# A 3x3 convolution with residual: combined images pair columns instead of rows

## The chip, the cores and the metric

The kernel runs on one core of a Trainium2 chip. The metric is the device time of one launch in microseconds (us); lower is better. TensorE (PE) does the matmuls, with its weight loads shown as PEld; VectorE is DVE, ScalarE is ACT, GpSimd is POOL, and SP issues most of the DMAs.

## What is computed

There are 160 images of 128 channels and 32 x 32 pixels. Each is normalised in groups of four channels, convolved with a 3x3 kernel of 128 x 128 channels, and added to itself. There are five sets of weights; 32 images use each. The weights are first quantised in two steps.

```python
s1 = (beta - alpha) / 3.0
v1 = s1 * floor(U / s1)
s2 = s1 / 5.0
v2 = s2 * floor((U - v1) / s2)
w = (v1 + v2).reshape(OUT_CH * N, IN_CH, 3, 3)
xb = x.reshape(B // N, N * C, H, W)
act = conv_general_dilated(xb, w, strides (1, 1), padding 1, groups N)
...
m = mean(g, axis=(2, 3, 4)); s = var(g, axis=(2, 3, 4))   # 32 groups
gn = (g - m) / sqrt(s + 1e-5)
...
x = x + conv(gn(x), U)
```

## The kernel before

The weights are whole numbers in fp16; an image is split into a high and a low fp16 part, and both are multiplied. Channels lie on the 128 partitions. An image's output fills two PSUM banks of 512 fp32 each (`eo`), the upper and the lower 16 rows.

The convolution saves products along the rows. For a pair of neighbouring output rows three vertical taps (g0, g1, g2) need four products instead of six: two "main" ones on differences of rows two apart (with g0 and with -g2), and two "sums", of g0+g1+g2 with the sum of a row pair and of g0-g1+g2 with its difference. Each product is made once for each of the three columns of taps, with the image shifted by one column, so two of three matmuls work on rows of 31. The sums of image i+1 go to the banks `m1a` or `m1b` and `m2`, ahead of image i's main part. `leave` copies `m2` to SBUF on ACT, `pairs` writes m1+m2 and m1-m2 into the rows of a new `eo` on DVE, and the main products are then accumulated on top. Taps are stored doubled, so `eo` holds twice the result, and `residual` halves it.

There are two kinds of image from the seventh on. In a **plain** image the high part is convolved directly (`taps`, L660: 9 taps x 2 halves = 18 matmuls); only the low part takes the short way (L699: 12 main products of 8 rows each, 6 sums). In a **combined** image differences and sums are made from the raw fp32 image into `v` of 2048 elements (`outer_rows` on POOL for the two edge rows, `combine` on DVE for the rest), scaled and split afterwards into `vh` (ACT, L607) and `vl` (DVE, L613); both parts take the short way: 24 main products and 12 sums, 36 matmuls, as many as the 18 + 12 + 6 of a plain image. There are 82 combined images and 75 plain ones of this kind; the first three use taps alone. Up to image 126 the two kinds alternate.

The order on every engine is written out by hand in `run`: an iteration i holds the sums of i+1 and the main part of i on PE, the low part of i+2, the normalisation of i+3 and the edge rows of i+4, then `pairs` of i+1 and `combine` of i+4 on DVE. Statistics of later images run on ACT (L194, L201), with short chains on POOL (L220 to L245). `residual` on ACT (L788) evacuates `eo` into `sum`, and POOL issues a DMA that adds `sum` to the image in SBUF (L807); 23 images take one DVE instruction instead (L799). Weights of the next set are quantised on DVE a step at a time; a finished column of taps is turned on PE (`turn_column`), copied by ACT (`keep_taps`, `keep_halves`) and combined by POOL (`keep_sums`). The products' matmul is a single line:

```python
self.nc.tensor.matmul(
    target[:, :, c0:c1],
    self.wts[n, col][:, kind, :],
    source[:, :, c0 + dw : c1 + dw],
```

Of the kernel before, what the change touches and what calls it, by code (L numbers as in the profile page):

```python
# [33 lines left out]
class Steps:  # L34
# [61 lines left out]
    def nearest(self, pool, v, parts, name, dt, by_scalar=False):  # L96

        tag = "ns" if by_scalar else "nn"
        n = pool.tile(list(v.shape), dt, tag=tag, name=f"{tag}_{name}")
        engine = self.nc.scalar.mul if by_scalar else self.nc.vector.tensor_scalar_mul  # L100
        engine(n, v, parts[0])
        return n
# [208 lines left out]
class Main:  # L311
# [35 lines left out]
    G, SUM, DIFF, MINUS_G2 = slice(0, 3), 3, 4, 5  # L347

    def __init__(self, tc, ctx, keep, x, u, out):
# [41 lines left out]
        self.wts = {}  # L391
# [91 lines left out]
    def keep_taps(self, n, col):  # L483

        P = self.P
        wt = self.wpool.tile([P, 6, P], MM, tag=f"wt{col}", name=f"wt{n}_{col}")
        self.nc.scalar.mul(wt[:, self.G, :], self.pt, 2.0 / LIFT)  # L487
        self.wts[n, col] = wt

    def keep_halves(self, n, col):  # L490
        half = self.qpool.tile([self.P, ROW, self.P], MM, tag="half", name=f"half{n}_{col}")
        self.nc.scalar.mul(half, self.pt, 1.0 / LIFT)
        return half

    def keep_sums(self, n, col, half):

        nc, P, wt = self.nc, self.P, self.wts[n, col]
        outer = self.qpool.tile([P, P], MM, tag="outer", name=f"outer{n}_{col}")
        nc.gpsimd.tensor_tensor(outer, half[:, 0, :], half[:, 2, :], ALU.add)
        nc.gpsimd.tensor_tensor(wt[:, self.SUM, :], outer, half[:, 1, :], ALU.add)  # L500
        nc.gpsimd.tensor_tensor(wt[:, self.DIFF, :], outer, half[:, 1, :], ALU.subtract)
        nc.gpsimd.tensor_scalar_mul(wt[:, self.MINUS_G2, :], wt[:, 2, :], -1.0)

    def keep_column(self, n, col):
        self.keep_taps(n, col)
        self.keep_sums(n, col, self.keep_halves(n, col))
# [71 lines left out]
    def outer_rows(self, i):  # L578

        nc, P, H, W = self.nc, self.P, self.H, self.W  # L580
        st, j = self.column_of(i)
        v = self.v[i] = self.wide.tile([P, 2048], F32, tag="v", name=f"v{i}")
        x = self.image(i)
        minus, last = st.ngm[:, j], (H - 1) * W
        nc.gpsimd.tensor_scalar(v[:, :W], x[:, W : 2 * W], minus, -1.0, ALU.add, ALU.mult)  # L585
        nc.gpsimd.tensor_scalar(
            v[:, last : H * W], x[:, last - W : last], minus, 1.0, ALU.add, ALU.mult
        )

    def combine(self, i):  # L590


        nc, H, W = self.nc, self.H, self.W
        st, j = self.column_of(i)
        v, x, last = self.v[i], self.image(i), (H - 1) * W
        nc.vector.tensor_sub(v[:, W:last], x[:, : last - W], x[:, 2 * W :])  # L596
        pairs = x.rearrange("p (i a w) -> p a i w", a=2, w=W)
        s, t = (v[:, k : k + 512].rearrange("p (i w) -> p i w", w=W) for k in (1024, 1536))
        nc.vector.scalar_tensor_tensor(
            s, pairs[:, 0], st.twice[:, j], pairs[:, 1], ALU.add, ALU.add  # L600
        )
        nc.vector.tensor_sub(t, pairs[:, 1], pairs[:, 0])  # L602
# [24 lines left out]
    def combinations(self, i):  # L627


        nc, P, H, W = self.nc, self.P, self.H, self.W  # L630
        lo = self.los[i % len(self.los)]
        rows = self.v[i] = self.rows.tile([P, 2048], MM, tag="rows", name=f"rows{i}")
        d, st = self.halves(rows)
        yield nc.vector.tensor_sub(d, lo[:, 0:H, :], lo[:, 2 : H + 2, :])
        pairs = lo[:, 1 : H + 1, :].rearrange("p (i a) w -> p a i w", a=2)
        yield nc.vector.tensor_add(st[:, 0], pairs[:, 0], pairs[:, 1])
        yield nc.vector.tensor_sub(st[:, 1], pairs[:, 1], pairs[:, 0])

    def halves(self, v):

        return (
            v[:, :1024].rearrange("p (h w) -> p h w", w=self.W),
            v[:, 1024:].rearrange("p (a i w) -> p a i w", a=2, w=self.W),
        )

    def taps(self, i, part, col, target, last, halves=(0, 1)):
# [7 lines left out]
        for k in (1, 0, 2):  # L654
            for h in halves:

                h0 = h * (H // 2)
                r0, r1 = max(h0, 1 - k), min(h0 + H // 2, H + 1 - k)
                s0 = r0 + k - 1 + top
                nc.tensor.matmul(  # L660
                    self.bank(target, h)[:, r0 - h0 : r1 - h0, c0:c1],
                    self.wts[n, col][:, k, :],
                    tile[:, s0 : s0 + r1 - r0, c0 + dw : c1 + dw],
                    start=(i < self.FIRST and col == self.COLS[0] and k == 1 and top == 0),
                    stop=(last and k == 2),
                    skip_group_check=True,
                )
# [17 lines left out]
    def direct_hi(self, i, col):  # L685
# [3 lines left out]
        self.taps(i, (self.hi[i], 0), col, self.eo[i], False)  # L689

    def direct_lo(self, i, col):
        lo = self.los[i % len(self.los)]
        self.taps(i, (lo, 1), col, self.eo[i], col == self.COLS[-1])

    def product(self, target, i, kind, source, col, start, stop):
        n, _ = self.place(i)
        dw = col - 1
        c0, c1 = max(0, -dw), self.W - max(0, dw)
        self.nc.tensor.matmul(  # L699
            target[:, :, c0:c1],  # L700
            self.wts[n, col][:, kind, :],
            source[:, :, c0 + dw : c1 + dw],
            start=start,
            stop=stop,
            skip_group_check=True,
        )
# [4 lines left out]
    def both(self, i):  # L711

        return [self.halves(v) for v in ([self.hi[i]] if self.combined(i) else []) + [self.v[i]]]

    def sums_of_pairs(self, i):

        both = self.both(i)
        for a, kind in ((1, self.DIFF), (0, self.SUM)):
            for col in self.COLS:
                for j, (_, st) in enumerate(both):  # L720
                    self.product(
                        self.m2_ps if a else self.m1(i), i, kind, st[:, a], col,
                        col == self.COLS[0] and j == 0,
                        col == self.COLS[-1] and j == len(both) - 1,
                    )

    def conv(self, i, on_the_way):
# [4 lines left out]

        for halves in ((0,), (1,)) if i == self.imgs - 1 else ((0, 1),):
            for col in self.COLS:
                if col == self.COLS[2] and i == self.FIRST:
                    self.sums_of_pairs(i + 1)
                if col != self.COLS[0] and halves[-1] == 1:
                    on_the_way(col)
                self.rest_of_column(i, col, halves)
        del self.v[i]  # L740

    def rest_of_column(self, i, col, halves):
        eo, both = self.eo[i], self.both(i)
        if not self.combined(i):
            self.taps(i, (self.hi[i], 0), col, eo, False, halves)
        for a, kind in enumerate((0, self.MINUS_G2)):
            for j, (d, _) in enumerate(both):
                for h in halves:
                    rows = slice(h * 16 + a, h * 16 + 16, 2)
                    to = eo[:, h].rearrange("p (i a) w -> p a i w", a=2)[:, a]  # L750
                    self.product(
                        to, i, kind, d[:, rows, :], col, False,
                        col == self.COLS[-1] and a == 1 and j == len(both) - 1,
                    )

    def leave(self, i):

        m2 = self.evac.tile([self.P, self.H // 2, self.W], F32, tag="m2", name=f"m2_{i}")
        self.nc.scalar.copy(m2, self.m2_ps)  # L759
        self.m2[i] = m2  # L760

    def pairs(self, i, between=lambda: None):
# [5 lines left out]
        rows = eo.rearrange("p h (i a) w -> p (h i) a w", a=2)  # L768
        nc.vector.tensor_add(rows[:, :, 0], m1, m2)  # L769
        between()  # L770
        nc.vector.tensor_sub(rows[:, :, 1], m1, m2)  # L771
# [8 lines left out]
    def residual(self, i):  # L780
# [5 lines left out]
        if not self.by_hand(i):  # L786
            self.sum[i] = self.sums.tile([self.P, 1024], F32, tag="sum", name=f"sum{i}")
            nc.scalar.mul(self.sum[i], eo.rearrange("p h r w -> p (h r w)"), 0.5)  # L788
            return
        xj = self.image(i)  # L790
        if i == self.imgs - 1 or eo is self.pair:
            parts = [
                (slice(h * 512, h * 512 + 512), self.bank(eo, h).rearrange("p r w -> p (r w)"))
                for h in range(2)
            ]
        else:
            parts = [(slice(0, 1024), eo.rearrange("p h r w -> p (h r w)"))]
        for h, part in parts:
            nc.vector.scalar_tensor_tensor(  # L799
                xj[:, h], part, 0.5, xj[:, h], ALU.mult, ALU.add  # L800
            )
            if i >= self.imgs - LAST:
                nc.sync.dma_start(self.ov[n, :, b, h], xj[:, h])
# [12 lines left out]
    def run(self):  # L816
# [120 lines left out]
        half = self.keep_halves(0, self.COLS[2])  # L937
        self.stats[2].deviations()
        self.keep_sums(0, self.COLS[2], half)
# [5 lines left out]
        for i in range(self.imgs):  # L945
# [58 lines left out]
            else:  # L1004
# [14 lines left out]
                if self.combined(i + 4):  # L1019
                    self.outer_rows(i + 4)  # L1020
# [98 lines left out]
```

## Time and profile before

| | |
|---|---|
| Time, median of 3 runs | 989.86 us (989.83 to 991.1) |
| Span of the profiled execution | 988.9 us (its own time isn't listed apart from the three above) |
| PE busy | 955.3 us, 97%, 5938 matmuls |
| PEld busy | 577.8 us, 58% |
| DVE busy | 933.8 us, 94%, 1259 instructions |
| ACT busy | 891.7 us, 90%, 1219 instructions |
| POOL busy | 414.9 us, 42%, 569 instructions |
| Mean DMA rate | 249 GB/s |
| Mean granted TensorE clock | 0.998 |

The busy shares are of the span. A busy PE is not PE at its peak: matmuls are pipelined, and their ends are modelled, so a matmul's price is read from the distance between starts or from the chain of waits, not from its duration. Groups of instructions are named by line, engine, output and inputs; idle time stands behind the bar, with what ended it.

### The profile page before, as it was taken

Reading aid. Unit: us, or ns where it says so; the run is one execution under the profiler, and the core shown is the slowest. Engines: PE = TensorE matmul, PEld = TensorE weight load, DVE = VectorE, ACT = ScalarE, POOL = GpSimd, SP = SyncE. Lnnn points to the kernel's source line nnn. Section 1 sums busy time; section 2 is a strip of 40 time slices with the busy share of each in tenths; the row PEclk is TensorE's granted clock in tenths of the full one; section 3 lists DMA queues with packets and bytes.
Section 4 is the critical chain, followed back from the end, with each engine's and each line's share of the span. In section 5 each row is a group of like instructions: output and inputs, shape, how many; then the busy total and the mean of one; then the engine's idle time right before and its main releaser. Section 6 shows DMA issues by size and latency. Waiting matters only on the chain.

```text
span 988.9 us, 16124 instructions
## 1 busy us (share of the span) xinstructions
PE 955.3 (97%) x5938; PEld 577.8 (58%) x5938; DVE 933.8 (94%) x1259; ACT 891.7 (90%) x1219; POOL 414.9 (42%) x569
## 2 busy tenths in 40 slices
PE   2899999999999999999999999999999999999997
PEld 1445656566656566666666666666665556666664
DVE  7999999999999999999999999999999999989995
ACT  5779999899999999999999999999999999998651
POOL 4435564634416273514343736415343544332410
PEclk9999999999999999999999999999999999999999
DMA  9538999999997989998998898998999899987764
GB/s 360 209 104 235 238 251 280 252 267 266 268 302 183 296 215 297 267 288 243 271 239 267 224 274 232 315 271 246 233 280 301 212 293 224 298 231 207 184 177 153
DMA packets 65129, 246.05 MB, mean 249 GB/s; under 512 B 5008, under 2 KB 5008, under 8 KB 65040
## 3 DMA queue, kind: packets, MB, share of 16 engines
q1 hardware_dynamic: 45312, 173.09, 50.3%
q0 software_dynamic: 19728, 71.84, 37.7%
q8 instruction: 48, 0.79, 0.3%
q14 instruction: 41, 0.34, 0.1%
HBM read 89.19 MB, written 83.89 MB: 175 GB/s over the span
## 4 chain that ended last, share of the span: by engine, by line
PE 66%; ACT 12%; DVE 10%; issue 5%; POOL 3%; DMA 3%; SPq 0%; DVEq 0%; ACTq 0%; POOLq 0%
PE eo L699 22%; PE eo L660 21%; PE m L699 11%; PE m1b L699 7%; PE m1a L699 4%; ACT junk L201 3%; ACT vh L607 3%; ACT sum L788 2%; ACT z L538 1%; DVE v L596 1%; DMA xt<-sum 1%; ACT m L759 1%; DVE vl L613 1%; DVE eo L769 1%; POOL v L585 1%
## 5 line engine op out<-in xcount | busy, mean ns | idle before, releaser
L699 PEld LDWEIGHTS <-wt 128*128 128x128 f16 x4302 | 420.4, 98 | 236.5 <-issue 4.1
L660 PE MATMUL eo<-hi,wt 128*128 128x496 f16 (+3 forms) x1386 | 331.0, 375 | 1.6 <-ACT wt L487 0.9
L807 POOL DMA_DIRECT2D xt<-sum x137 | 122.8, 906 | 441.1 <-ACT sum L788 426.9
L660 PEld LDWEIGHTS <-wt 128*128 128x128 f16 x1458 | 142.5, 99 | 138.4 <-DVE eo L771 2.3
L613 DVE SCALAR_TENSOR_TENSOR vl<-v,rstd,vh 128x2048 f16<-128x2048 f32 x82 | 192.9, 2352 | 1.9 <-ACT vh L607 1.9
L699 PE MATMUL eo<-vh,wt 128*128 128x248 f16 (+1 forms) x984 | 188.5, 273 | 0.0
L699 PE MATMUL eo<-vl,wt 128*128 128x248 f16 (+1 forms) x984 | 188.5, 273 | 0.0
L194 ACT ACTIVATE junk<-xt 128x1024 f16<-128x1024 f32 x152 | 160.6, 1057 | 18.0 <-DMA xt<-in_x_dram 14.2
L201 ACT ACTIVATE junk<-xt,mv 128x1024 f16<-128x1024 f32 x152 | 173.8, 1143 | 0.1
L607 ACT ACTIVATE vh<-v,rstd 128x2048 f16<-128x2048 f32 x82 | 164.8, 2009 | 4.7 <-DVE v L602 2.4
L788 ACT ACTIVATE sum<-eo 128x1024 f32<-128x1024 f32 x137 | 138.2, 1008 | 14.0 <-PE eo L699 14.0
L699 PE MATMUL eo<-rows,wt 128*128 128x256 f16 (+1 forms) x900 | 135.3, 273 | 0.0
L759 ACT COPY m<-m 128x512 f32<-128x512 f32 x157 | 90.7, 578 | 19.2 <-PE m L699 19.1
L538 ACT ACTIVATE z<-xt,shift,rstd 128x1024 f32<-128x1024 f32 x75 | 93.6, 1248 | 3.5 <-POOL shift L243 3.4
L620 DVE TENSOR_TENSOR lo<-z,hi 128x1024 f16<-128x1024 f32 x78 | 95.6, 1225 | 0.0
L699 PE MATMUL m<-vl,wt 128*128 128x496 f16 (+1 forms) x246 | 93.4, 380 | 1.1 <-DVE vl L613 1.1
L699 PE MATMUL m<-vh,wt 128*128 128x496 f16 (+1 forms) x246 | 93.4, 380 | 1.0 <-ACT m L759 1.0
L596 DVE TENSOR_TENSOR v<-xt 128x960 f32<-128x960 f32 x82 | 94.3, 1150 | 0.0
L585 POOL TENSOR_SCALAR v<-xt,ngm 128x32 f32<-128x32 f32 x82 | 90.7, 1106 | 0.1
L553 ACT CAST hi<-z 128x1024 f16<-128x1024 f32 x78 | 81.6, 1046 | 2.3
L699 PE MATMUL m1b<-vh,wt 128*128 128x496 f16 (+1 forms) x213 | 80.9, 380 | 0.0
L699 PE MATMUL m1b<-vl,wt 128*128 128x496 f16 (+1 forms) x213 | 80.9, 380 | 0.0
(129 smaller groups left out, 1210.0 us busy)
## 6 DMA issues: line engine op xcount, KB each, us to landing
xt<-in_x_dram SPq DMA_DIRECT2D x78, 1024.0 KB, 9.5
out_dram<-xt SPq DMA_DIRECT2D x78, 1024.0 KB, 5.9
xt<-sum POOLq DMA_DIRECT2D x137, 512.0 KB, 6.5
u<-in_L_conv_U_dram SPq DMA_DIRECT2D x4, 576.0 KB, 9.6
xt<-in_x_dram SPq DMA_DIRECT2D x4, 512.0 KB, 9.6
range<-in_L_conv_U_dram SPq DMA_DIRECT2D x3, 576.0 KB, 7.8
out_dram<-xt SPq DMA_DIRECT2D x3, 512.0 KB, 2.8
u<-in_L_conv_U_dram SPq DMA_DIRECT2D x2, 288.0 KB, 2.9
```

Of the source, the lines that this page charges most:

```text
L194: self.nc.scalar.activation(junk, image, ACTF.Copy, scale=-1.0 / image.shape[1], accum_out=self.mv[:, j, 0:1],)
L201: self.nc.scalar.activation(junk, image, ACTF.Square, bias=self.mv[:, j, 0:1], accum_out=self.mv[:, j, 1:2],)
L538: nc.scalar.activation(z, self.image(i), ACTF.Identity, bias=st.shift[:, j : j + 1], scale=st.rstd[:, j : j + 1],)
L585: nc.gpsimd.tensor_scalar(v[:, :W], x[:, W : 2 * W], minus, -1.0, ALU.add, ALU.mult)
L596: nc.vector.tensor_sub(v[:, W:last], x[:, : last - W], x[:, 2 * W :])
L607: self.nc.scalar.mul(vh, self.v[i], st.rstd[:, j])
L613: self.nc.vector.scalar_tensor_tensor(vl, self.v[i], st.rstd[:, j], self.hi[i], ALU.mult, ALU.subtract)
L660: nc.tensor.matmul(self.bank(target, h)[:, r0 - h0 : r1 - h0, c0:c1], self.wts[n, col][:, k, :], tile[:, s0 : s0 + r1 - r0, c0 + dw : c1 + ...
L699: self.nc.tensor.matmul(target[:, :, c0:c1], self.wts[n, col][:, kind, :], source[:, :, c0 + dw : c1 + dw], start=start, stop=stop, skip_g ...
L759: self.nc.scalar.copy(m2, self.m2_ps)
L788: nc.scalar.mul(self.sum[i], eo.rearrange("p h r w -> p (h r w)"), 0.5)
L807: self.nc.gpsimd.dma_start(self.image(i), self.sum.pop(i), accum_op=ALU.add)
```

## The change

Combined images now pair neighbouring columns, with the three rows of taps as the shifts. `v` is stored so that a quarter (even outputs, odd outputs, sums, differences) holds 32 rows of 16 column pairs; a shift by one row is then a shift by 16 elements, and a shifted product is one contiguous run of 496. The weights of sums and differences across columns are a new tile, `across`, made once for each set when its last column is kept. Plain images keep pairing rows, but the two banks of `eo` now hold even and odd output rows (for combined images: columns) instead of halves, so that a main product fills a whole bank. The sign of the odd differences moves from the weights into the differences. The taps are stored plain, not doubled; the factor of a half goes into `leave` and `pairs`. `residual` puts even and odd outputs back in their places as it evacuates. The last image's products are ordered by bank, and it is stored after both banks.

```diff
     def keep_taps(self, n, col):
-        wt = self.wpool.tile([P, 6, P], MM, ...)
-        self.nc.scalar.mul(wt[:, self.G, :], self.pt, 2.0 / LIFT)
+        wt = self.wpool.tile([P, 5, P], MM, ...)
+        self.nc.scalar.mul(wt[:, self.G, :], self.pt, 1.0 / LIFT)
...
-    def keep_halves(self, n, col):
-        half = self.qpool.tile([self.P, ROW, self.P], MM, ...)
-        self.nc.scalar.mul(half, self.pt, 1.0 / LIFT)
-        return half
...
-        nc.gpsimd.tensor_tensor(outer, half[:, 0, :], half[:, 2, :], ALU.add)
-        nc.gpsimd.tensor_tensor(wt[:, self.SUM, :], outer, half[:, 1, :], ALU.add)
-        nc.gpsimd.tensor_tensor(wt[:, self.DIFF, :], outer, half[:, 1, :], ALU.subtract)
-        nc.gpsimd.tensor_scalar_mul(wt[:, self.MINUS_G2, :], wt[:, 2, :], -1.0)
+    def both_sums(self, total, diff, g0, g1, g2):
+        pool = self.nc.gpsimd
+        pool.tensor_tensor(total, g0, g2, ALU.add)
+        pool.tensor_tensor(diff, total, g1, ALU.subtract)
+        pool.tensor_tensor(total, total, g1, ALU.add)
+    def keep_sums(self, n, col):
+        wt = self.wts[n, col]
+        self.both_sums(wt[:, self.SUM], wt[:, self.DIFF], *(wt[:, k] for k in range(ROW)))
+        if col == self.COLS[-1]:
+            across = self.wpool.tile([self.P, 2, ROW, self.P], MM, ...)
+            self.across[n] = across
+            self.both_sums(
+                across[:, 0], across[:, 1], *(self.wts[n, c][:, self.G] for c in range(ROW))
+            )
...
-        nc.gpsimd.tensor_scalar(v[:, :W], x[:, W : 2 * W], minus, -1.0, ALU.add, ALU.mult)
-        nc.gpsimd.tensor_scalar(
-            v[:, last : H * W], x[:, last - W : last], minus, 1.0, ALU.add, ALU.mult
-        )
+        self.nc.gpsimd.tensor_scalar(
+            self.view(v, 0, (512 + W // 2 - 1, 2), (W // 2, H)),
+            self.view(self.image(i), 1, (W - 3, 2), (W, H)),
+            st.ngm[:, j], -1.0, ALU.add, ALU.mult,
+        )
...
-        nc.vector.tensor_sub(v[:, W:last], x[:, : last - W], x[:, 2 * W :])
-        nc.vector.scalar_tensor_tensor(
-            s, pairs[:, 0], st.twice[:, j], pairs[:, 1], ALU.add, ALU.add
-        )
-        nc.vector.tensor_sub(t, pairs[:, 1], pairs[:, 0])
+        nc.vector.tensor_tensor(
+            self.view(v, 1, (511, 2), (half, H), (1, half - 1)),
+            self.view(x, 1, (1, 2), (W, H), (2, half - 1)),
+            self.view(x, 3, (-3, 2), (W, H), (2, half - 1)),
+            ALU.subtract,
+        )
+        even, odd = (x[:, a::2] for a in range(2))
+        nc.vector.scalar_tensor_tensor(
+            v[:, 1024:1536], even, st.twice[:, j], odd, ALU.add, ALU.add
+        )
+        nc.vector.tensor_sub(v[:, 1536:], odd, even)
...
     def product(self, target, i, quarter, step, kind, start=False):
+        for j, source in enumerate(self.both(i)):
+            source = source[:, quarter * 512 : quarter * 512 + 512]
+            if self.combined(i):
+                weights = self.across[n][:, kind - self.SUM, step] if kind >= self.SUM else (
+                    self.wts[n, kind][:, step]
+                )
+                out, half = target.rearrange("p i w -> p (i w)"), W // 2
+                first, end = max(0, -shift) * half, 512 - max(0, shift) * half
+                out, moving = out[:, first:end], source[:, first + shift * half : end + shift * half]
...
+    def main(self, i, a, between=lambda: None):
+        to = self.bank(self.eo[i], a)
+        for step in self.KS:
+            if step == self.KS[1] and a == 1 or step == self.KS[2] and a == 0:
+                between()
+            if not self.combined(i):
+                self.taps(i, (self.hi[i], 0), step, self.eo[i], (a,))
+            self.product(to, i, a, step, 2 * a)
...
-        self.nc.scalar.copy(m2, self.m2_ps)
+        self.nc.scalar.mul(m2, self.m2_ps, 0.5)
...
-        nc.vector.tensor_add(rows[:, :, 0], m1, m2)
+        nc.vector.scalar_tensor_tensor(eo[:, 0], m1, 0.5, m2, ALU.mult, ALU.add)
         between()
-        nc.vector.tensor_sub(rows[:, :, 1], m1, m2)
+        nc.vector.scalar_tensor_tensor(eo[:, 1], m1, 0.5, m2, ALU.mult, ALU.subtract)
...
+    def as_banks(self, i, image):
+        if self.combined(i):
+            return image.rearrange("p (q a) -> p a q", a=2)
+        return image.rearrange("p (i a w) -> p a i w", a=2, w=self.W)
...
-            nc.scalar.mul(self.sum[i], eo.rearrange("p h r w -> p (h r w)"), 0.5)
+            nc.scalar.copy(self.as_banks(i, self.sum[i]), self.flat(i, eo))
...
+            for a, quarters in ((0, (slice(0, 512),)), (1, (slice(0, 256), slice(256, 512)))):
+                for h, q in enumerate(quarters):
+                    nc.vector.tensor_add(image[:, a, q], banks[:, a, q], image[:, a, q])
+                    if a == 1:
+                        half = slice(h * 512, h * 512 + 512)
+                        nc.sync.dma_start(self.ov[n, :, b, half], xj[:, half])
```

Three smaller edits go with it: `combinations` writes its differences by even and odd rows, `taps` takes every second row, and a scratch tile of the quantisation shares a buffer with another.

## The prediction

> **What bounds the kernel now.** I read the page's busy shares first, then the engines' busy time in one long steady stretch (200 to 800 us; after the stretch's length come PE, PEld, DVE, ACT, POOL), then the chain of waits inside it, and last the groups of instructions with shapes kept apart.
>
> ```profile
> PE 955.3 (97%) x5938; PEld 577.8 (58%) x5938; DVE 933.8 (94%) x1259; ACT 891.7 (90%) x1219; POOL 414.9 (42%) x569
> ```
> ```profile
> 200.00:800.00 600.00, 598.95 (x3751) 364.44 (x3749) 577.27 (x764) 582.69 (x800) 259.63 (x341) 1.00 0.94 261
> ```
>
> TensorE is busy 599 of 600 us at full granted clock, so it sets the pace; but DVE has 577 and ACT 583 of the same 600, and both are close behind. The chain of waits between 500 and 515 us is TensorE alone:
>
> ```profile
> 504.22 2.63 PE eo L699 x24
> 506.84 1.30 PE m L699 x6
> 508.14 1.30 PE m1b L699 x6
> 509.44 1.27 PE eo L660 x6
> 510.70 0.44 PE eo L699 x4
> 511.14 1.27 PE eo L660 x6
> 512.41 0.44 PE eo L699 x4
> 512.85 1.27 PE eo L660 x6
> 514.12 0.44 PE eo L699 x4
> 514.56 0.65 PE m L699 x3
> 515.21 0.65 PE m1a L699 x3
> 515.86 2.63 PE eo L699 x24
> ```
>
> One combined image (24 main products, 12 sums) and one plain image follow each other, and the pattern repeats from 504.22 to 515.86: 11.64 us for a pair. In that period ACT works 582.69/600 x 11.64 = 11.30 us and DVE 11.20 us, so ACT has 0.34 us to spare and DVE 0.44 us. The steps also price a matmul. 24 narrow products (8 rows of 32 or 31 columns) take 2.63 us: 109.4 ns each. Six wide ones (one of 512, then rows of 31) take 1.30 us: 216 ns each, although two thirds of them have only 496 columns. The six taps at 509.44 are four of 512 and two of 480: (1270 - 4 x 216)/2 = 203 ns for 480. So 32 columns fewer are worth 13.5 ns, **a row of 31 costs as much as a row of 32**, and a contiguous 496 should cost 216 - 13.5/2 = 209 ns.
>
> [...] So two halves cost only 2.5 to 3 ns more than one whole: fewer matmuls is by itself nearly worthless. [...] one L585 of 32 elements ran from 176.82 to 182.14 us[...], where it takes 0.30 us at 54.70.
>
> **The change part by part.**
>
> *Main products.* Per combined image 24 narrow ones become 12: 4 of 512 (216) and 8 of contiguous 496 (209) = 2.54 us, from 2.63: -0.09. *Sums*, 12 as before, but flat: 2.54 from 2.59: -0.05. Together -0.14 us x 82 images = **-11.6 us**. Per plain image 12 narrow products (3 x 0.44) become 6 wide with rows of 31 (6 x 216 = 1.30): -0.016 x 75 = **-1.2 us**. The taps keep count and shape; they read every second row, as the narrow products do now at no cost. All of it lies on the path: **-12.8 us** if the other engines follow; zero if the 496 gained nothing and the halves were free.
>
> *DVE.* The two writes of `pairs` become scalar_tensor_tensor with an immediate. L769/L771 take 695 ns for 512; L799, such an instruction out of PSUM, took 687: no difference. The plain `combinations` keep their counts and unit inner step. `combine` keeps its 960 + 512 + 512 elements but reads every second element, in runs of 15. I take its present 1149 + 746 + 684 ns. Its rows fit 1.03 ns an element at both lengths, so a gain isn't in sight; above, twice that would be +2.1 us per combined image, five times DVE's spare.
>
> *ACT.* `leave` gets a scale (L759, 578 ns for 512; L788 with a scale 1008 for 1024: same slope). `residual` loses its scale, and for 65 of 137 images writes every second element. I take 1008 ns; twice the 0.84 ns per element would be 1.87. 15 `keep_halves` of 481 ns go: -7 us of ACT work, beside PE.
>
> *POOL.* `outer_rows`' two instructions (1106 + 906 ns[...]) become one of 64 elements. But its outputs now lie between those of `combine`, and the built order shows that the first subtraction of `combine` **waits for POOL**, which L596 does not. Behind it stand the rest of `combine`, the next low part and the next `pairs`, for which PE waits. In the trace L586 ended after L596 began in 12 of 82 cases, in a few more within 0.05 us of it; in the others it was done, typically 0.12 us earlier, and one instruction fewer adds about 0.3 us. In the late cases POOL was behind two DMA issues or statistics and started at about L596's start or up to 0.9 us before it: 0.3 to 0.6 us of stall each[...]: 4 to 7 us of DVE time in all, most of it inside DVE's 0.44 us per pair.
>
> *Weights.* Per column POOL has three chained instructions of 128 for four (L499 to L502); the last column of a set gets three more of 384. From 0.20 us for 4 elements and 0.43 for 128, 384 take about 0.9; with the gaps +2.7 us per set. At the start this is on the path, as the chain shows:
>
> ```profile
> 51.02 0.43 POOL L499 TENSOR_TENSOR outer<-half 128x128 f16<-128x128 f16 x1
> 51.53 0.43 POOL L500 TENSOR_TENSOR wt<-outer,half 128x128 f16<-128x128 f16 x1
> 51.92 0.43 POOL L501 TENSOR_TENSOR wt<-outer,half 128x128 f16<-128x128 f16 x1
> 52.31 0.53 POOL L502 TENSOR_SCALAR wt<-wt 128x128 f16<-128x128 f16 x1
> 52.81 1.04 POOL L236 TENSOR_TENSOR rstd<-ve,mhalf 128x4 f32<-128x4 f32 x1
> ```
> ```profile
> 54.58 1.24 ACT L538 ACTIVATE z<-xt,shift,rstd 128x1024 f32<-128x1024 f32 x1 [1.07 <-POOL shift L243]
> ```
>
> rstd moves 2.7 us back, and z, the evacuation at 56.80, `pairs` and the first PE main part at 58.90 with it; up to three `keep_halves` of 0.38 us on the same early chain go. I take **+1.5 us** (0 to 2.7). At the four later set changes the cover is the two or three images between the last column and its first use; for image 128, combined and the first of its set, it is about 5 us against about 4.5 of undisturbed POOL work, and L501 there took 2.47 us. I take **+1.5** for all four (0 to 8).
>
> *Less slack.* With a pair at 11.48 us, ACT (11.21 without `keep_halves`) and DVE (11.20) keep 0.27. Before, PE was idle 3.5 of the 800 us from 100 to 900, at 96% of DVE and ACT; at 97.5%, with POOL waits, I take **+2.5** (1 to 5).
>
> *The end.* The last image's DVE work already starts after the last matmul (982.44). Three additions for two, the first store after the second: **+0.2**. SP has no other change.
>
> Sum: -12.8 + 1.5 + 1.5 + 2.5 + 0.2 = -7.1 us. The profiled span is 988.9; the median of three runs is 989.86, so about 1 us lies outside the span, and the profiled execution's own time isn't listed apart. 989.9 - 7.1 = **982.8**; by the bounds 977 to 993.
>
> **The rivals.**
>
> *ACT's store at every second element is slow* (slower). ACT has 0.34 us plus 0.09 from `keep_halves`: from 0.43 us more, 1.44 us per `sum` instead of 1.01, it ends the pair and the kernel is slower than before. At twice per element a pair takes 11.21 + 0.86 = 12.07: 65 x 0.43 = +28 us, **1018**. For it: ACT is at 97%, and the trace has no strided store. [...]
>
> *`combine` is slow* (the same mechanism on DVE, decided from 22% on its 1984 elements): at twice 13.3 us a pair, 80 x 1.6 = +130 us, near 1120. Less likely, as its short rows now read free (L636, 32-element rows, 438 ns for 512).
>
> *The saving is hidden.* DVE and ACT in turn hold PE back; only a fifth is left: **988 to 990**. For it: the 96 to 97%, and the DVE steps in the chain near 795 to 809. Against: 599 of 600.
>
> *It does not do what it says:* contiguous 496 costs 216 after all. Then only -4 us from the halves, against +5.7: **992**.
>
> **How the numbers follow.** Forecast 0.62; hidden saving 0.16; 496 at 216 with the same waits 0.09; strided ACT or DVE 0.13. About 0.2% (2 us) is what a measurement can tell from no change. Faster by more: most of the forecast (0.58) and a third of the hidden case, some of the last two: 0.65. Within: 0.11. Slower: strides and the bad ends of the waits, 0.24. The likeliest case alone spans 977 to 990. The range runs from 976 to 1004, into a mild stride cost; the doubled ones are left out.
>
> **What would show it.** In the profile after: six flat sums in 1.27 us instead of 1.30, a combined image in 5.08 and a pair near 11.48 us; `sum` at 1.0 us on ACT; `combine` at 1.15 + 0.75 + 0.69; DVE waits on POOL of a few us in all; the first main part near 60.4 us. A `sum` of 1.4 us or more, a `combine` over 3 us, or PE under 97% busy from 200 to 800 would prove it wrong.

## Result and profile after

The changed kernel is **slower by 0.27%**: 992.61 us (median of 11 runs, 991.02 to 995.6) against 990.27 us for the kernel before on the same chip (11 runs); ratio 1.0027, 95% interval 1.0017 to 1.0037. The prediction was 982.8, with 0.65 on faster. Below, "against the changed kernel" means the difference of two such ratios times 990 us, so that runs on different chips compare; the changed kernel stands at +2.7 us by this. Such a difference is good to 1 or 2 us: the interval of the changed kernel alone is 1.0 us to either side, and one kernel timed on two chips (e5, e16) differs by 2.0.

The profiled execution of the kernel after took 992.18 us, its span is 990.4. From its page, the busy shares, and two groups (line, engine, shapes, count | busy us, mean ns | idle before, and what ended it):

```profile
PE 947.1 (96%) x4504; PEld 440.5 (44%) x4504; DVE 934.8 (94%) x1260; ACT 889.9 (90%) x1204; POOL 382.1 (39%) x487
...
L810 ACT COPY sum<-eo 128x1024 f32<-128x1024 f32 x137 | 141.6, 1033 | 11.1 <-PE eo L725 11.0
...
L605 DVE TENSOR_TENSOR v<-xt 128x960 f32<-128x960 f32 x82 | 94.8, 1156 | 11.9 <-POOL v L593 11.9
```

TensorE has its 1434 matmuls less and is busy 8 us less. The same stretch of 200 to 800 us as before (length; then PE, PEld, DVE, ACT, POOL):

```profile
200.00:800.00 600.00, 592.10 (x2826) 275.26 (x2824) 575.99 (x761) 579.75 (x790) 253.73 (x290) 1.00 0.94 262
```

TensorE now stands idle 7.9 us of the 600, where it was 1.05. The chain of waits over one pair of images shows the saving as planned:

```profile
503.81 2.54 PE eo L725 x12
506.35 1.27 PE m L725 x6
507.62 1.27 PE m1b L725 x6
508.89 0.64 PE eo L670 x3
...
514.00 0.65 PE m L725 x3
514.64 0.65 PE m1a L725 x3
515.29 1.91 PE eo L725 x9
```

A combined image takes 2.54 + 1.27 + 1.27 = 5.08 us, and an undisturbed pair 515.29 - 503.81 = 11.48. So the matmuls do what was predicted, and the time was lost elsewhere. Where it was lost is read off by comparing each start-to-start distance of TensorE with the undisturbed one for its width (216 ns for 512, 209 for contiguous 496) and adding up the excess by stage:

| TensorE's excess, us | 40 us to image 5 | images 5 to 127 | 127 to 131 | 131 to the end | sum |
|---|---|---|---|---|---|
| before | 3.4 | 9.0 | 0.8 | 1.8 | 15.0 |
| after | 7.2 | 13.9 | 4.6 | 3.4 | 29.1 |

The rows come from one execution of each kernel. About 5 us of the second column, in both rows, are the short stops behind the statistics matmuls. The excess grew by 14.1 us and the span by 1.5, so the matmuls gave 12.6 (predicted 12.8), and more than all of it went back.

**The start.** The chain of the kernel after:

```profile
51.40 0.88 POOL across L494
52.28 0.07 issue
52.35 0.92 POOL across L495
53.27 0.07 issue
53.34 0.91 POOL across L496
54.25 1.00 POOL rstd L236
...
61.04 0.94 ACT hi L559
61.99 0.03 issue
62.01 0.36 PE small L209 x2
62.37 0.76 PE eo L670 x3
63.13 0.43 PE eo L725
```

Three `across` instructions stand ahead of rstd, as expected. Not expected is the end: the first main part waits for L209, a statistics matmul. In `conv` the first of these images makes its `on_the_way` work ahead of the main part, where before it stood behind the first column of taps, and L209 needs statistics and image data that DVE and ACT finish only at 61.92 and 61.98. TensorE is idle from 58.0 to 62.0. The banks of the main part are ready from `pairs` at 60.25, so 1.9 us of this are L209's. Then three L670 take 0.76 us and one L725 takes 0.43: for eight matmuls the distance is about 426 ns instead of 216, since TensorE's granted clock is halved for 3.4 us (0.50 from 63 to 66 us).

How long it stays halved differs from one execution to another. Variants whose start is the same as here (e3, e4, e6, e7, e8, e15, below) show 3.4 us in one trace and 6.8 in five. From 61 to 69 us, first after, then e7 (the number behind the five engines is the share of full clock):

```profile
61.00:69.00 8.00, 6.99 (x26) 2.99 (x27) 7.83 (x15) 3.72 (x7) 0.71 (x4) 0.79 0.32 110
61.00:69.00 8.00, 6.86 (x21) 2.91 (x22) 7.10 (x13) 2.67 (x7) 0.00 (x0) 0.58 0.30 105
```

e7's excess up to image 5 is 8.3 us, so the 7.2 of the table is a mild case.

**Image 128**, the first of the last set and a combined one:

```profile
791.95 2.93 POOL across L494
794.88 0.07 issue
794.95 0.91 POOL across L495
...
797.43 0.67 POOL v L593
798.10 0.02 issue
798.12 1.16 DVE v L605
```

```profile
PEld L725 <- POOL across L495: 2.9, 1, 2.9
```

The first fence is the chain, the second the list of waits between 792 and 797 us (engine and line, what it waited for, us, times, longest). L494 took 2.93 us instead of 0.9 (DVE's `vl` ran from 791.58 to 794.09; whether it held L494 up isn't shown), TensorE's weight load waited for `across` while TensorE stood idle for 2.4 us, and again about eight matmuls at double distance followed (413 to 427 ns, at a granted clock of 0.50 from 797 to 800 us).

**In between**, the page shows DVE waiting 11.9 us for POOL's outer columns (L605 on L593), which I first took for the cause of the rest.

### The profile page after: what moved, and what is told of

It reads as the page before. It is cut to its first block, busy times and chain, and to the rows that moved or that the text cites. A ratio compares the mean times of both kernels' runs of the same rounds, so it can differ in the third digit from the quotient of the medians.

```text
span 990.4 us, 13240 instructions
## 1 busy us (share of the span) xinstructions
PE 947.1 (96%) x4504; PEld 440.5 (44%) x4504; DVE 934.8 (94%) x1260; ACT 889.9 (90%) x1204; POOL 382.1 (39%) x487
## 4 chain that ended last, share of the span: by engine, by line
PE 42%; DVE 20%; ACT 17%; issue 9%; POOL 8%; DMA 4%; DVEq 0%; SPq 0%; POOLq 0%; ACTq 0%
PE eo L725 14%; PE eo L670 14%; PE m L725 7%; PE m1b L725 5%; ACT junk L201 4%; ACT vh L620 4%; DVE v L605 3%; POOL rstd L236 3%; DMA xt<-in_x_dram 2%; PE m1a L725 2%; ACT sum L810 2%; DVE vl L626 2%; ACT z L544 2%; DVE eo L782 2%; DVE lo L633 2%
## 5 line engine op out<-in xcount | busy, mean ns | idle before, releaser
L670 PE MATMUL eo<-hi,wt 128*128 128x496 f16 (+2 forms) x1386 | 369.3, 377 | 0.9 <-ACT wt L488 0.9
L725 PEld LDWEIGHTS <-wt 128*128 128x128 f16 x1884 | 183.2, 99 | 214.7 <-DVE eo L784 7.8
L670 PEld LDWEIGHTS <-wt 128*128 128x128 f16 x1458 | 142.8, 99 | 166.2 <-issue 2.0
L725 PE MATMUL eo<-vh,wt 128*128 128x496 f16 (+1 forms) x492 | 184.5, 375 | 3.7 <-DVE eo L784 3.7
L725 PE MATMUL eo<-vl,wt 128*128 128x496 f16 (+1 forms) x492 | 184.4, 375 | 0.0
L194 ACT ACTIVATE junk<-xt 128x1024 f16<-128x1024 f32 x152 | 160.6, 1056 | 21.1 <-DMA xt<-in_x_dram 17.6
L725 PE MATMUL eo<-rows,wt 128*128 128x496 f16 (+1 forms) x450 | 171.6, 381 | 0.0
L810 ACT COPY sum<-eo 128x1024 f32<-128x1024 f32 x137 | 141.6, 1033 | 11.1 <-PE eo L725 11.0
L725 PEld LDWEIGHTS <-across 128*128 128x128 f16 x984 | 96.3, 98 | 122.5 <-issue 10.4
L773 ACT ACTIVATE m<-m 128x512 f32<-128x512 f32 x157 | 93.4, 595 | 22.3 <-PE m L725 22.2
L605 DVE TENSOR_TENSOR v<-xt 128x960 f32<-128x960 f32 x82 | 94.8, 1156 | 11.9 <-POOL v L593 11.9
L725 PE MATMUL m<-vl,across 128*128 128x496 f16 (+1 forms) x246 | 92.6, 376 | 3.7 <-DVE vl L626 3.5
L725 PE MATMUL m<-vh,across 128*128 128x496 f16 (+1 forms) x246 | 92.5, 376 | 3.3 <-ACT junk L194 2.4
L593 POOL TENSOR_SCALAR v<-xt,ngm 128x64 f32<-128x64 f32 x82 | 81.6, 996 | 0.2 <-DVE vl L626 0.2
L725 PE MATMUL m1b<-vl,across 128*128 128x496 f16 (+1 forms) x213 | 79.9, 375 | 0.0
```

The lines of the kernel that those rows point to most:

```text
L194: self.nc.scalar.activation(junk, image, ACTF.Copy, scale=-1.0 / image.shape[1], accum_out=self.mv[:, j, 0:1],)
L605: nc.vector.tensor_tensor(self.view(v, 1, (511, 2), (half, H), (1, half - 1)), self.view(x, 1, (1, 2), (W, H), (2, half - 1)), self.view(x ...
L670: nc.tensor.matmul(self.bank(target, a)[:, first:end, c0:c1], self.wts[n, col][:, k, :], tile[:, s0 : s0 + 2 * (end - first) - 1 : 2, c0 + ...
L725: self.nc.tensor.matmul(out, weights, moving, start=start and j == 0, stop=False, skip_group_check=True)
L773: self.nc.scalar.mul(m2, self.m2_ps, 0.5)
L810: nc.scalar.copy(self.as_banks(i, self.sum[i]), self.flat(i, eo))
```

## Experiments

Sixteen variants, each timed beside the kernel before. The theory at first: three places (start, image 128, POOL's late outer columns). Rivals: DVE and ScalarE have no slack to follow a faster TensorE anywhere; ScalarE's store at every second element hides the saving.

| Run | us, median | ratio to before (95%) | against the changed kernel |
|---|---|---|---|
| e1_order | 991.03 | 1.0005 (0.9998 to 1.0012) | -2.2 |
| e2_late | 989.13 | 0.9986 (0.9979 to 0.9993) | -4.1 |
| e3_outer | 993.53 | 1.0034 (1.0025 to 1.0043) | +0.7 |
| e4_split | 993.65 | 1.0028 (1.0016 to 1.0040) | +0.1 |
| e5_all | 984.80 | 0.9942 (0.9929 to 0.9955) | -8.4 |
| e6_thin | 984.75 | 0.9942 (0.9928 to 0.9957) | -8.4 |
| e7_light | 984.09 | 0.9938 (0.9925 to 0.9950) | -8.8 |
| e8_straight | 993.43 | 1.0028 (1.0018 to 1.0037) | +0.1 |
| e9_start | 988.31 | 0.9982 (0.9972 to 0.9992) | -4.5 |
| e10_start_outer | 987.46 | 0.9966 (0.9952 to 0.9979) | -6.0 |
| e11_start_split | 988.82 | 0.9985 (0.9978 to 0.9993) | -4.2 |
| e12_share | 989.12 | 0.9990 (0.9982 to 0.9998) | -3.7 |
| e13_start_light | 979.73 | 0.9897 (0.9882 to 0.9913) | -12.9 |
| e14_before_light | 986.63 | 0.9960 (0.9947 to 0.9974) | -4.0 against before |
| e15_whole | 998.49 | 1.0083 (1.0069 to 1.0098) | +5.5 |
| e16_all_again | 986.39 | 0.9962 (0.9949 to 0.9976) | -6.4 |

### The start: e1, e2, e9

```diff
# e1: the statistics matmul inside the main part
-            on_the_way(self.COLS[1])
-            self.main(i, 0)
+            self.main(i, 0, lambda: on_the_way(self.COLS[1]))
# e2: the first set's `across` after the scales of images 4 to 7
-        self.keep_sums(0, self.COLS[2])
+        self.keep_sums(0, self.COLS[2], across_too=False)
...
+                    self.keep_across(0)
```

> In the changed kernel the statistics matmul, which waits for DVE and ScalarE work that ends near 61.9 us, stands ahead of image 3's first main part in TensorE's queue; here it stands between that part's second and third step, as for every other image. Theory of the three places (the start, image 128, POOL's late outer columns): the first main part starts near 60.3 instead of 62.0 us, the idle before it falls from 4.2 to about 2.5 us, and if the half clock that followed (10 matmuls at 426 ns instead of 216, 2 us) comes only with the longer idle, it goes too: 2 to 4 us faster than the changed kernel, 988.5 to 990.5. If the short idle still halves the clock: 1.5 us faster. Rival, slack on DVE and ScalarE (a late start is caught up by the engines that lead, or an early one is lost again to them): less than 0.7 us at the end, 992.

> The three POOL instructions for `across` of the first set (0.91 us each) are made after the scale and shift of images 4 to 7 rather than ahead of them. Theory of the three places: rstd returns to near 52.8 us, the evacuation of m2 to 56.8, the end of the first pair of banks to about 58.9; but the first main part stays behind the statistics matmul in TensorE's queue, so it starts only as much earlier as that matmul's DVE operand does (0.5 to 1.4 us): 0.5 to 2 us faster than the changed kernel. If `across` was the whole delay at the start: 3 us or more. Rival, slack on DVE and ScalarE: less than 0.7 us, 992.

> Only the two edits at the start, of e1 and e2 together. Singly they took TensorE's extra idle before image 5 from 3.8 us (7.2 against 3.4 before) to 1.8 and to -0.5. Together: -0.5 to -1, so little beyond e2: 988 to 989.5. If the 5 us that the four edits brought beyond the sum of the single ones come from these two: 984.5 to 986.

e1 gave 2.2 us and e2 4.1, which is more than I had given it, and even past the 3 us set for `across` as the whole delay. But e1 wins with `across` in its place, so neither is the whole. The chain of e2:

```profile
51.69 1.04 POOL rstd L236
...
58.52 0.95 ACT hi L562
59.47 0.03 issue
59.49 0.35 PE small L209 x2
59.85 0.65 PE eo L673 x3
```

rstd starts 2.56 us earlier than after, L209 2.52, and three L673 now take 0.65 us: the slow matmuls are gone. They are gone in e1 too, where the first main part starts at 60.66. The idle that is left in front is 1.4 us in e2 and 2.3 in e1. The excess up to image 5 is 5.3 us in e1, 3.0 in e2 and 2.7 with both (e9); e9 gained 4.5 us. So the start is a cause by itself. The gains of e1 and e2 don't add up, as each of them also removes the slow matmuls.

### Image 128: e4, e11

```diff
+        if n == N_SETS - 1:
+            self.across_by_parts(n, col)   # g0+g1, g0-g1 early; +g2 first
```

> For the last set the sums across columns are made in two steps, g0+g1 and g0-g1 after the second column and the addition of g2 to both as soon as the third is there and ahead of that column's own sums. Theory of the three places: `across` for image 128 is ready some 2 us earlier than 795.9, TensorE's wait of 2.6 us before image 128's sums goes, with the half clock after it (about 2 us) and the late outer columns of image 132: 3 to 5.5 us faster, 987 to 989.5. [...] Rival, slack: what is gained at image 128 is lost again by 160, since ScalarE and DVE set the pace there: less than 1.5 us.

> The two edits at the start, and the last set's `across` in parts. In e4 and e5 the parts took TensorE's idle around image 128 from 4.6 to 2.8 and 2.3 us: 1.8 to 2.3 us less than the start edits alone, 986 to 987.5. If the gain at 128 is lost again by the end, within 0.7 us of them.

The parts did in the trace what they should: no wait for `across` in e4, and the excess from 127 to 131 falls from 4.6 to 2.8 us, in e11 from e9's 4.6 to 2.8. The time did not follow (+0.1, and +0.3 against e9). In e4, at the sums of image 130, TensorE waited 1.6 us for a `vl` of DVE:

```profile
PE m L741 <- DVE vl L642: 1.6, 1, 1.6
```

The late `across` is a real wait, but behind it DVE is late for TensorE by part of the same amount. What it costs in time isn't settled; alone, not 4 us.

### POOL's outer columns: e3, e10

```diff
+                if self.combined(i + 4):
+                    self.outer_columns(i + 4)
                 if i > self.FIRST and self.by_hand(j):
...
                     self.accumulate(j)
-                if self.combined(i + 4):
-                    self.outer_columns(i + 4)
```

> The outer columns of image i+4 are issued on POOL ahead of the two residual additions' DMA issues of the same step rather than behind them. Theory of the three places: DVE's wait for them (11.9 us in 13 places) falls to 3 us or less, TensorE's waits for `pairs` by 4 to 6 us, and the end by 3 to 5 us: 988 to 990. If the later DMA issue holds image buffers longer, a part comes back as waits for loads. Rival, slack: DVE has the time to spare and the waits of TensorE come from DVE and ScalarE at 96 to 97% of the pace, so the wait only moves to another instruction: within 1 us of the changed kernel. Rival, the store at every second element: no change either.

> The two edits at the start, and the outer columns ahead of the DMA issues. Alone the latter took DVE's waits for POOL from 11.9 us to nothing and left TensorE's idle in the middle where it was. If that holds here too: the time of the start edits alone within 1 us. If DVE's waits for POOL matter once the start is repaired: 2 to 4 us less than those.

From the list of waits of e3, 60 to 985 us:

```profile
POOL v L593 <- DVE vl L626: 28.1, 7, 8.9
DVE eo L782 <- ACT m L773: 21.1, 28, 3.6
...
DVE v L605 <- POOL v L593: 2.2, 1, 2.2
```

DVE's waits for POOL fell from 11.9 us to one of 2.2, and its waits for ACT's `m` rose from 12.5 in the list of after to 21.1. TensorE's excess between images 5 and 127 stayed at 13.6 us (13.9), and the time at +0.7. **My theory of the third place fell**: without DVE's waits for POOL, TensorE stops elsewhere for as long. From 350 to 500 us its idle fell from 1.5 us to 0.3, from 200 to 350 it rose from 1.2 to 3.0. With the start repaired, e10 stands 1.5 us below e9, and their intervals overlap.

### Who sets the pace in between: e6, e7, e14, e8

```diff
# e6: one low product fewer in the difference sums
-        for j, source in enumerate(self.both(i)):
+        for j, source in enumerate(self.both(i)[:1] if kind == self.DIFF and step == 2 else self.both(i)):
# e7 (in the kernel before: e14): DVE's third instruction of combine
-        nc.vector.tensor_sub(v[:, 1536:], odd, even)
+        nc.vector.tensor_copy(v[:, 1536:], x[:, :512])
# e8: ACT's `sum` in plain order
-            nc.scalar.copy(self.as_banks(i, self.sum[i]), self.flat(i, eo))
+            nc.scalar.copy(
+                self.sum[i].rearrange("p (a i w) -> p a (i w)", a=2, w=self.W),
+                eo.rearrange("p a i w -> p a (i w)"),
+            )
```

> One product of 496 columns (the low part, third step) is left out of the difference sums of each of the 82 combined images: 82 x 0.209 = 17.1 us less work for TensorE, nothing else changes. If TensorE still sets the pace of the changed kernel: 17 us faster, about 975.5, with the same idle times. If DVE and ScalarE now share the pace (they have 0.27 us of 11.48 to spare, and this takes 0.21 more): most of the 17 us returns as TensorE's waits for `pairs`, `vl` and `m2`; 3 to 8 us faster than the changed kernel, 984 to 990, TensorE near 97% busy from 200 to 800.

> The third instruction of `combine` (two inputs in SBUF, 0.70 us, 80 times) becomes a copy of 512 contiguous elements with one input; the differences of the pairs are left out. If it takes 0.3 to 0.6 us, DVE gets 8 to 30 us less work in all[...]. If DVE's missing slack holds TensorE back in the middle stretch (5 us more idle than before there): 3 to 6 us faster than the changed kernel, and those idle times gone. If ScalarE is the one that can't follow: less than 1.5 us. The delay at the start stays in either case.

> The same copy in the kernel before the change (the differences of the pairs are left out). There TensorE stood idle for 9.0 us between images 5 and 127, 4.9 of it the short stop behind each statistics matmul, which no relief of DVE takes away. If TensorE set the pace before, and the change made DVE's slack the limit: 1.5 to 4 us faster than before, 986 to 988.5, against 8.5 in the changed kernel. If DVE was the limit before as well: 7 us or more.

> ScalarE's `sum` of combined images is stored in plain order rather than at every second element; the interleaving of the output is left out. The 65 stores should fall from 1.08 to 0.99 us each, 5.5 us of ScalarE time. If the slower store hides the saving (ScalarE sets the pace in the middle): 3 to 5 us faster than the changed kernel. If DVE does, or the waits sit at single places: less than 1.5 us.

e6 took 17.1 us of work from TensorE and won 8.4. e7 took nothing from TensorE and 23 us from DVE (82 copies of 421 ns for subtractions of 701), and won 8.8. The stretch from 200 to 800, first of e6, then of e7:

```profile
200.00:800.00 600.00, 589.71 (x2815) 273.48 (x2814) 586.44 (x771) 587.67 (x799) 250.77 (x290) 1.00 0.95 265
```
```profile
200.00:800.00 600.00, 595.99 (x2851) 278.46 (x2849) 567.96 (x768) 585.57 (x797) 232.16 (x290) 1.00 0.95 264
```

With less to do, TensorE is idle more (10.3 us); with a lighter DVE it is idle 4.0 us, 2.6 of them at image 128, and from 300 to 785 us it stops for nothing but statistics. In e7 DVE still waited 8.6 us for POOL, so those waits are harmless once DVE has time to spare. With the copy POOL was busy 232 us of the 600 against 254, too; what that gave can't be told from DVE's own time, but e3, where POOL was busy 238 us and nothing was won, suggests that it is small. What ended TensorE's stops ahead of the main parts in the same stretch, first after, then e7, was `pairs` on DVE (us, times, longest):

```profile
PE eo L725 <- DVE eo L784: 3.7, 6, 1.2
```
```profile
PE eo L725 <- DVE eo L784: 0.4, 1, 0.4
```

In the kernel before, the same copy (e14) won 4.0 us: DVE already held TensorE back there a little, and the change doubled it. **Compared with a light DVE on both sides, and the start repaired, the change is worth 0.9897 - 0.9960, or -6.2 us.** e8 gave nothing, though ACT's stores fell as meant:

```profile
L810 ACT COPY sum<-eo 128x1024 f32<-128x1024 f32 x137 | 136.3, 995 | 11.2 <-PE eo L725 11.0
```

Why DVE, which averages 96%? A part of the answer was in the kernel before. Two stretches of 30 us in which a column of the next set's weights is quantised, first before, then after:

```profile
365.00:395.00 30.00, 30.00 (x186) 17.89 (x184) 29.80 (x41) 28.86 (x41) 13.95 (x17) 1.00 1.00 274
555.00:585.00 30.00, 30.00 (x184) 17.85 (x183) 29.76 (x41) 28.20 (x40) 11.66 (x18) 1.00 1.00 280
```
```profile
365.00:395.00 30.00, 29.66 (x142) 13.54 (x139) 28.99 (x39) 28.61 (x40) 9.53 (x13) 1.00 0.99 278
555.00:585.00 30.00, 29.53 (x141) 13.49 (x139) 29.76 (x43) 27.44 (x37) 8.16 (x13) 1.00 1.00 286
```

Before, DVE was busy 29.8 of 30 us there and just kept TensorE at 30.00; after, TensorE is idle there for 0.34 and 0.47 us. But these two stretches hold little of the loss. The longest stop of the middle, 1.3 us, stands at 434 us, where DVE is busy for 91% only (first before, then after, then the chain of after):

```profile
412.00:445.00 33.00, 33.00 (x203) 19.58 (x201) 31.05 (x38) 31.83 (x45) 8.89 (x18) 1.00 1.00 288
412.00:445.00 33.00, 31.83 (x152) 14.60 (x150) 29.91 (x39) 31.75 (x43) 17.17 (x19) 1.00 0.96 272
```
```profile
424.99 0.90 POOL xt L833
425.89 0.43 POOL v L593
426.32 0.02 issue
426.35 1.16 DVE v L605
...
431.30 1.15 DVE xt L827
...
433.31 0.71 DVE eo L784
434.02 0.05 issue
434.06 2.08 PE eo L725 x9
```

Here DVE had waited for POOL's outer columns behind a DMA issue, and made one of its own residual additions (L827) on top. So e7 and e14 show that DVE holds TensorE back; that the weight columns are the main reason isn't shown. Weight columns, residual additions and waits for POOL each use up what DVE has to spare, and their shares stay open.

### Separate causes, and the worth of the narrow products: e13, e15

e13 is e9 with the copy of e7; e15 is an edit of its own:

```diff
# e15: no shift, all products 512 wide
-                out, moving = out[:, first:end], source[:, first + shift * half : end + shift * half]
...
+                moving = source
```

> The two edits at the start, and the third instruction of `combine` as a copy of 512 elements (the differences of the pairs are left out), as in e7. If the start (4.3 us) and DVE's slack in the middle and the end (8.5 us) are separate causes: 12 us faster than the changed kernel, 979 to 981, with TensorE's idle only around image 128. If the light DVE merely caught up the late start: 983 to 985.

> The products of combined images all read and write 512 columns; the shift by a column is left out. 16 products per combined image go from 496 to 512 columns, 7 ns each: 82 x 16 x 7 = 9.2 us more work for TensorE. If TensorE sets the pace of the changed kernel: 9 us slower than it, about 1001.5. If DVE and ScalarE share the pace: 3 to 6 us slower, 995.5 to 998.5. If contiguous 496 costs as much as 512: no change.

e13 won 12.9 us, e9's 4.5 and e7's 8.8 added (13.3): two causes, not one seen twice. e15 put 9.2 us of work back on TensorE and cost 5.5: contiguous 496 is cheaper than 512 in time as well, but not at full worth, since part of its gain is waited away. e6, in the other direction, says the same.

### A better kernel: e5, e16, e12

e5 and e16 are the four edits of e1 to e4 together; e12 adds:

```diff
-        return i > self.BY_VECTOR[-1] - 4 and i % 8 == 7
+        return i > self.BY_VECTOR[-1] - 4 and i % 16 == 7
```

> The four edits together: statistics matmul inside the first main part, first `across` after the scales, outer columns ahead of the DMA issues, last set's `across` in parts. Singly they gave -1.6, -3.5, +0.9 and +1.0 us against the changed kernel's 992.6. If the places are separate (TensorE's idle at the start, at image 128), the start gives 4 to 5 us and image 128 another 1 to 2.5: 986 to 988, about 3 us faster than before. If DVE and ScalarE set the pace through the middle and the end, an earlier start is kept (they start earlier too), but the gain at 128 is lost again by the end: 988 to 989.5.

> The four edits again, beside the others on one chip. If e5's 984.8 was the kernel's level: 984 to 986. If it was a lucky draw of few executions: 987 to 988.5, as the start edits alone.

> All four edits, and every second of the residual additions that DVE makes (1.22 us each, 8 images of 16) goes to ScalarE (a `sum` of 1.0 or 1.08 us and a DMA). DVE gets 9.8 us less work, ScalarE 8.4 more. If DVE's slack is what TensorE still waits for: 1.5 to 3 us faster than the four edits alone, 982 to 983.5. If ScalarE is as short: no change, or 1 to 3 us slower.

Twice the four edits beat both kernels: 0.58% and 0.38% below before. How much the outer columns and the parts add to the start isn't certain, since e10, e11 and e16 lie within 2 us of e9 (e5 lies 3.9 below it). e12 moved 9.8 us from DVE to ACT and lost 2.7 us or more against the four edits: ACT, at 97%, has nothing to spare either, and e8 only shows that its 5.5 us were not what TensorE waited for.

## Why the prediction was wrong

- *Main products and sums, plain images: right.* 12.8 us predicted, 12.6 measured; the distances 209 and 216 ns, 5.08 and 11.48 us stand in the chain.
- *Edits costed at nothing: right but for one.* `combine` took 1156 + 754 + 701 ns (1149 + 746 + 684 assumed), `pairs` 695 to 700, `leave` with its scale 595. ACT's store at every second element took 1078 ns against 993 in plain order: 8.5% more, where the prediction assumed no cost, which nothing in the trace of before showed, and the rival twice the time per element. It cost nothing in time (e8), so **that rival is refuted**, as is `combine`'s.
- *The start: mis-sized.* 1.5 us predicted, 3.8 measured in the excess of one execution (about 5 where the half clock lasted 6.8 us), and 4.5 to be had by repairing it. The delay of rstd was sized well (z 1.4 us later). What the step lacked was the order on PE: I followed POOL and ACT and not the statistics matmul that the new `conv` puts ahead of the main part, though the diff shows it. The first main part came at 62.2 us, not 60.4. The slow matmuls after the idle, 1.7 us or more, came on top.
- *Set changes: the place was right.* Image 128 was named, and L494 took 2.93 us as L501 had taken 2.47. The wait with what followed is 3.8 us more than before, against 1.5 for all four sets (up to 8); its worth in time stays open.
- *Less slack: the step that failed.* 2.5 us predicted. The excess grew by 4.9 us in the middle and 1.6 at the end, and a lighter DVE wins 8.8 us here against 4.0 before. The sum took a mean of 0.27 us to spare per pair and the 3.5 us that TensorE had lost at 96% as the measure of the waits; but DVE comes late in single places, and then TensorE stops for it (`pairs`). At the weight columns it was 99% busy in the trace that I had; how much of the 6.5 us they make isn't shown. With the start, the set changes and the end, costs put at 5.7 us together came to 14.1. "PE under 97% busy" was the wrong alarm: 98.7% was enough to lose.
- *The end:* 0.2 predicted, part of the 1.6 above.
- *POOL's waits:* larger than foreseen (11.9 us of DVE time in 13 places against 4 to 7, the author's estimate), and yet e3, without them, was no faster: they use up what DVE has to spare, as other things do.
- *The rivals.* "The saving is hidden" had the mechanism, with 0.16, and stopped at 988 to 990: it left out that the costs at the start and at image 128 come on top of a hidden saving. "It does not do what it says" gave the closest number (992) for a reason that e15 refutes.

## What to carry to other kernels

When one engine is at 99% and the next two at 96 to 97%, a mean to spare says little. Follow each stop of the first engine back along its chain, and make one of the others lighter in a trial, on both sides of the change: e7 and e14 told more than the busy time of any stretch, which was 99% in some and 91% where TensorE stopped longest. When a loop is restructured, list for each engine's queue what now stands ahead of the first critical instruction; a matmul of four columns held the first main part up by 1.9 us. And a wait that the profile shows in plain numbers (DVE on POOL, 11.9 us) is not a cause until removing it moves the end.

## What was not expected of the hardware

- After an idle of 4.0 to 4.3 us at the start, TensorE ran at half its clock in all seven traces that have it (granted 0.50 from 63 to 66 us in the kernel after, about 426 ns for 512 columns), for 3.4 us in two of them and for 6.8 in five. At image 128 it did so for 3.4 us after idles of 2.4 to 2.7 us in seven traces (after, e1, e2, e3, e7, e10, e13), and not at all after 2.40 us in e9 and 2.34 in e15. Near 41 us it did in e3, e15 and e16, after 1.9 us and a pause of 0.6 soon behind it, and not in e9 with the same two. So within 1.9 to 2.7 us the length of an idle doesn't decide it. What does isn't shown.
- ACT's fp32 store of 1024 elements took 1078 ns at every second element and 993 in plain order, 8.5% more. DVE's `combine`, with its reads at every second element, took 1156 + 754 + 701 ns against 1150 + 748 + 688 before, 1% more.
